# The second wave of read-back tiles placed behind the last single's loads, and its adds behind the last output

## The chip, the core and the metric

The kernel runs on one core of a Trainium2 chip. The metric is the device time of one execution in microseconds; several executions are made and the median is quoted. A profile of one further execution gives the times of single instructions; its times are counted from the start of its span.

## The reference, cut to what matters

Two layers are computed on 3327 nodes with 256 features each. A layer adds a graph convolution and then a mixture of experts to x. The end of layer 1, which is all that matters here, is this:

```python
out = tokens
for e in range(E):                                   # 8 experts, two of them chosen per token
    h = jax.nn.gelu(tokens @ w1[e] + b1[e], approximate=False)
    y = h @ w2[e] + b2[e]
    out = out + combine[:, e:e + 1] * y              # combine is zero but for the two chosen
...
x = x + _L1_ffn_ref((_layernorm(x, axis=-1))[None], ...)[0]
return x
```

Each token gets two weighted expert rows added to its row of x, and x is the result.

## The kernel before

The 3327 nodes are padded to 3328 and stand as 26 tiles of 128 rows; x stays in SBUF as [128, 26, 256]. The tokens are listed by expert in a table in DRAM (`xlist1`) and taken in blocks. A pair block has 256 tokens of one expert, a single has 128. Layer 1 runs 8 early pairs, 18 late pairs and, in the usual case, 6 singles: blocks 0 to 31 in the order in which they run, of which 26 to 31 are the singles. `layer1.step` runs a block: SP loads the tokens and the expert's first weights (lines 893, 900, 907, six blocks ahead), PE turns and multiplies them, ACT applies the GELU, PE multiplies again, and DVE adds the bias and scales by the token's weight (lines 987, 988). POOL then scatters the rows of the result to `ys1` in DRAM, one scatter for each 128 tokens (line 551). `ys1` has two rows for each token.

To finish, the two rows of every token are read back from `ys1` into the upper or lower part of a buffer of the ring (`load_outputs`, line 1050, issued by SP), DVE adds them to x in two instructions (`add_loaded`, line 1064), and x goes out to DRAM (lines 1384 and 1413). A read must not start before the scatters that fill its rows have landed. `follow` makes a read wait for a list of scatters; `outputs` holds all scatters so far. The blocks are planned so that tiles 0 to 13 have all their rows once 16 blocks are done, tiles 14 to 21 once 24 are done, and tiles 22 to 25 only with the last. (If a run's tokens don't fit this plan, another arm is taken, which the change doesn't touch.)

The loop over the steps (lines 1380 to 1402) places this work. `at` is the number of blocks begun. When `at` is 16 (`EARLY + E`), the seven pairs of tiles of the first wave are put in `waiting`, with the scatters of the first 16 blocks; when it is 24 (`EARLY + 2 * E`), the four pairs of tiles of the second wave (14 to 21), with those of the first 24. One read is placed per step, and the read is moved to `asked`; an add is placed two steps or more after its read, but, by the bound in the condition, not once `at` is over `layer1.always - FIXED[1]` = 26; the output follows a step later. The second wave's reads stand behind steps 27, 28, 29 and 30, and its adds come after the loop. There the four last tiles are read singly with all scatters as their list, and then all is added in the order of `asked`, then `left`; each add is followed by an output, from ACT, for the last tiles from ACT and SP in turn. `behind(last_y)` makes a scheduler place instructions behind the last scaling of an expert's rows on DVE.

Each engine runs its instructions in order. SP issues its transfers in order too: an instruction that waits holds up all that stand behind it. A DMA issued by SP, ACT or POOL goes on by itself and raises a semaphore when it has landed.

Of the kernel before, what the change touches and what calls it, by code (L numbers as in the profile page):

```python
# [25 lines left out]
D = 256  # L26
DC = D // P
E = 8
# [5 lines left out]
RING = 6  # L34
PIECE = CJ * PW
# [4 lines left out]
K = 2  # L40
# [18 lines left out]
EARLY = 8  # L59
# [5 lines left out]
FIXED = (4, 6)  # L65
# [13 lines left out]
BEGUN, FIRST_TILES, MORE_TILES = 12, 14, 22  # L79
# [12 lines left out]
def gnn_moe_two_layers(  # L92
# [24 lines left out]
    nc = tc.nc  # L117
# [12 lines left out]
    ring = [state.tile([P, PIECE], F32, name=f"ring{i}") for i in range(RING)]  # L130
# [93 lines left out]
    rows_written, early_rows, outputs, last_product, last_y = [], [], [], [], []  # L224
    after = mybir.DependencyInfo(mybir.DependencyClass.Sync, mybir.DependencyReason.DATA)

    def follow(later, earlier):
        for o in earlier:
            tc.add_manual_dep(later.ins, o.ins.name, after, reason="same rows of DRAM")

    def behind(instructions):

        if instructions and any(i is instructions[-1].ins for i in nc.cur_bb.bb.instructions):
            return tc.issue_after(instructions[-1].ins)
        return nullcontext()
# [31 lines left out]
    def statistics(t0, n, kept=None):  # L267


        mv, guess = kept or (  # L270
            work.tile([P, n, 2], F32, name="ln_mv"), work.tile([P, n], I32, name="ln_guess")
        )
        for g in range(n):
            st = work.tile([P, 6], F32, name="ln_st")
            nc.vector.bn_stats(out=st, in_=x[:, t0 + g, :])  # L275
            nc.vector.bn_aggr(out=mv[:, g, :], in_=st)
        ve = work.tile([P, n], F32, name="ln_ve")
        nc.vector.tensor_scalar(ve, mv[:, :, 1], EPS, None, ALU.add)  # L278
        nw = work.tile([P, n], F32, name="ln_nw")
        half = nw.bitcast(I32)  # L280
        nc.vector.tensor_scalar(half, ve.bitcast(I32), 1, None, ALU.logical_shift_right)
        nc.vector.tensor_scalar(guess, half, -1.0, float(0x5F3759DF), ALU.mult, ALU.add)
        rs = guess.bitcast(F32)
        for _ in range(3):
            nc.vector.scalar_tensor_tensor(nw, rs, -0.5, rs, ALU.mult, ALU.mult)
            nc.vector.tensor_tensor(nw, nw, ve, ALU.mult)
            nc.vector.scalar_tensor_tensor(rs, nw, 1.5, rs, ALU.add, ALU.mult)
        return mv, rs
# [149 lines left out]
    def rows_of(a, t0, n):  # L438
        return a[t0 * P : (t0 + n) * P, :].rearrange("(n p) d -> p n d", p=P)
# [609 lines left out]
    def load_outputs(yt, ys, t0, n, written, group=None):  # L1049
        d = nc.sync.dma_start(  # L1050
            out=yt,
            in_=ys[t0 * P * K : (t0 + n) * P * K, :].rearrange(
                "(n p k) d -> p n (k d)", p=P, k=K
            ),
        )
        follow(d, written)
        if group:
            tc.add_to_no_dep_group(group, d.ins)
        output_loads.append(d)

    def add_loaded(yt, t0, n):
        x_t = x[:, t0 : t0 + n, :]
        for k in range(K):
            nc.vector.tensor_tensor(x_t, x_t, yt[:, :, k * D : (k + 1) * D], ALU.add)  # L1064
# [10 lines left out]
    ys1 = dram.tile([YROWS, D], F32, name="ys1")  # L1075
# [110 lines left out]
    at = BEGUN * K * D  # L1186
# [15 lines left out]
    for t, n in FOURS:  # L1202
        if t < BEGUN:
            yt = in_s[:, t * K * D : (t + n) * K * D]
            begun.append((yt.rearrange("p (n d) -> p n d", n=n), t, n))

    def add_begun():
        for b in begun:
            add_loaded(*b)
# [44 lines left out]
    def between():  # L1254

        normal.clear()
        second.clear()
        waiting = []
        for pair in turned_pairs():
            waiting.append(pair)  # L1260
            if len(waiting) > 1:
                second_features(*waiting.pop(0))
        second_features(*waiting.pop(0))
        outputs.clear()
        rows_written.clear()

        for pan in range(ahead):
            n_loads = len(begun) + (NCHUNK if pan == 0 else 0)
            load_panel(pan, filter_behind, output_loads[0:n_loads])
# [22 lines left out]
    def new_layer1():  # L1292
        return experts(
            xlist1, ys1, "1", FIXED[1], D, AF.Gelu, f1_w1, f1_b1, f1_w2, f1_b2,
            nc.scalar.copy, kept=(EARLY // 2, w2_all, gate, f1_b1_sb),
        )
# [16 lines left out]
    def panels1(layer1, turn=False):  # L1313


        def after(pan):
            if pan < NPAN - 1:
                after1(layer1, pan)
                if turn and pan == NPAN - 2:
                    layer1.turn_first()  # L1320
            else:
                list_waiting()

        return after
# [23 lines left out]
    with tc.If(first_usual > 0) as arms:  # L1348
        output_loads.clear()
        for yt, t, n in begun:  # L1350
            load_outputs(yt, ys0, t, n, written, "read0")
        layer0.step(late)
        layer0.step(late)
        with behind(last_y):
            add_begun()
        layer0.step(late)
        with behind(last_y):
            statistics(0, BEGUN, begun_stats)
        layer0.steps_to(late, layer0.always)
        between()  # L1360
        layer1 = new_layer1()
        aggregate(gnn_b_sb, filter_chunk, panels1(layer1, True), loaded=ahead)
        late1 = first_blocks(layer1)

        layer1.steps_to(late1, EARLY - 1)
        layer1.step(late1, place=blk.tile([P, DC, SB], F32, name="xT_arms", bufs=1))
        baset, nbt = late1[4], late1[6]  # L1370
        second_usual = usual(
            [(FIRST_TILES, baset[:, E : 2 * E]), (MORE_TILES, baset[:, 2 * E :])],
            [(late1[5][0:1, :], FIXED[1])],
            nbt[:, E : 2 * E],
        )
        before_inner = layer1.state()
        with tc.If(second_usual > 0) as inner:  # L1377
            layer1.know(2 * E)
            waiting, asked, added, k = [], [], [], 0
            while len(layer1.started) < layer1.always:  # L1380
                layer1.step(late1)
                at = len(layer1.started)
                for tiles in added:
                    nc.scalar.dma_start(out=rows_of(out, *tiles), in_=x[:, tiles[0] : sum(tiles), :])
                added.clear()
                if at == EARLY + 2 * E - 2:
                    layer1.know_rest(late1)

                with behind(last_y):
                    if asked and asked[0][2] + 1 < at <= layer1.always - FIXED[1]:  # L1390
                        yt, tiles, _ = asked.pop(0)
                        add_loaded(yt, *tiles)
                        added.append(tiles)
                if waiting and at > waiting[0][1] + (1 if k < FIRST_TILES // 2 else 2):
                    tiles, _, written = waiting.pop(0)
                    yt = ring[k % RING][:, PIECE - 2 * K * D :].rearrange("p (n d) -> p n d", n=2)
                    load_outputs(yt, ys1, *tiles, written, "read1")
                    asked.append((yt, tiles, at))
                    k += 1
                if at in (EARLY + E, EARLY + 2 * E):  # L1400
                    tiles = range(0, FIRST_TILES, 2) if at == EARLY + E else range(FIRST_TILES, MORE_TILES, 2)
                    waiting.extend(((t, 2), at, list(outputs)) for t in tiles)
            assert not (waiting or added)
            left = []
            for i, t in enumerate(range(MORE_TILES, NT)):
                yt = ring[i][:, 0 : K * D].rearrange("p (n d) -> p n d", n=1)
                load_outputs(yt, ys1, t, 1, outputs)
                left.append((yt, (t, 1)))
            with behind(last_y):
                for i, (yt, tiles) in enumerate([(yt, tiles) for yt, tiles, _ in asked] + left):  # L1410
                    add_loaded(yt, *tiles)
                    queue = nc.sync if i > len(asked) and i % 2 else nc.scalar
                    queue.dma_start(out=rows_of(out, *tiles), in_=x[:, tiles[0] : sum(tiles), :])
        with inner.Else():
            layer1.back_to(before_inner)
            layer1.rest(late1)
            finish(FOURS)
    with arms.Else():
# [9 lines left out]
        layer1 = new_layer1()  # L1428
# [157 lines left out]
```

## Time and profile before

| | us |
|---|---|
| median of 7 runs | 1223.79 |
| lowest and highest of them | 1220.72, 1225.70 |
| profiled execution | 1224.16 |
| its span | 1222.44 |

The span reaches from the first to the last instruction; the execution's time is 1.72 longer. The stretches of the end, from a view that gives the busy time of each engine in each (us):

| stretch | PE | DVE | ACT | POOL | DMA share | GB/s |
|---|---|---|---|---|---|---|
| 1195 to 1198 | 2.94 | 1.02 | 1.66 | 1.68 | 0.19 | 69 |
| 1198 to 1209 | 4.63 | 6.03 | 1.86 | 3.38 | 0.84 | 272 |
| 1209 to 1217.5 | 0.00 | 5.08 | 0.00 | 0.00 | 0.78 | 241 |

SP has no row, since all it does is issue and wait. The DMA share is the mean busy share of the core's 16 DMA engines. In SP's own waits from 1193 on, most is for scatters:

```profile
SPq L1050 <- DMA ys<-wide,index: 13.2, 4, 4.2
```

The columns are the total, the number of waits and the longest one. A lowercase q behind an engine's name is its sequencer, which issues and waits.

### The profile page before, as it was taken

The numbers are of one execution on the slowest core, as the hardware profiler recorded it, in microseconds if no ns is written. First come the engines' busy times: TensorE is split into PE (matmuls) and PEld (weight loads), VectorE is DVE, ScalarE is ACT, GpSimd is POOL, SyncE is SP. The second block draws the span as 40 slices with busy tenths as digits, with TensorE's granted clock in tenths as the row PEclk, the third lists the DMA queues.
The fourth block names the chain that finished last, engine by engine and source line by source line (L and its number), as shares of the span: only waits on it lengthen the run. The fifth ranks groups of instructions, "written<-read, shape, count | busy, mean of one in ns | idle before, by whom it ended". The sixth has DMA issues, their size and how long they took to land. (4 is left out here: it accounts for less than half of the span.)

```text
span 1222.4 us, 18156 instructions
## 1 busy us (share of the span) xinstructions
PE 1190.0 (97%) x5819; PEld 1032.4 (84%) x5819; DVE 707.1 (58%) x2841; ACT 511.7 (42%) x950; POOL 270.2 (22%) x341
## 2 busy tenths in 40 slices
PE   8999999999999999999999999999999999999983
PEld 7888888888888888888888888888888888888862
DVE  7577756766583111111111177568999998886454
ACT  2655456545422222323222225896455453043321
POOL 3004111311141111011111110002323323255531
PEclk9999999999999999999999999999999999999997
DMA  9799744444358555756657657144445442477796
GB/s 342 175 311 287 214 147 169 148 156 154 100 182 263 182 185 179 262 177 225 219 194 237 230 198 283 66 168 176 163 179 187 161 170 87 122 247 231 231 290 209
DMA packets 123177, 241.59 MB, mean 198 GB/s; under 512 B 24480, under 2 KB 93120, under 8 KB 116160
## 3 DMA queue, kind: packets, MB, share of 16 engines
q1 hardware_dynamic: 108656, 205.59, 51.6%
q0 software_dynamic: 11136, 31.60, 7.1%
q10 hardware_dynamic: 3280, 3.15, 0.8%
q8 instruction: 48, 0.79, 0.3%
q14 instruction: 57, 0.47, 0.1%
HBM read 203.98 MB, written 36.33 MB: 197 GB/s over the span
## 5 line engine op out<-in xcount | busy, mean ns | idle before, releaser
L383 PE MATMUL ps_g<-ring,s 128*128 128x256 f32 x1352 | 297.0, 382 | 2.7 <-DVE s L297 2.6
L360 PE MATMUL ps_g<-s,ring 128*128 128x256 f32 x1352 | 294.2, 380 | 0.0
L383 PEld LDWEIGHTS ps_g<-ring,s 128*128 128x128 f32 x1352 | 257.5, 191 | 38.0 <-DVE s L297 3.7
L360 PEld LDWEIGHTS ps_g<-s,ring 128*128 128x128 f32 x1352 | 256.4, 190 | 33.9
L941 PE MATMUL ps_h<-xT,ring 128*128 128x256 f32 (+1 forms) x1176 | 249.3, 365 | 4.3 <-ACT xT L932 4.1
L941 PEld LDWEIGHTS ps_h<-xT,ring 128*128 128x128 f32 x1176 | 204.6, 190 | 41.3 <-ACT xT L932 5.2
L948 ACT ACTIVATE wide<-ps_h,ring 128x256 f32<-128x256 f32 (+1 forms) x240 | 110.2, 459 | 284.0 <-PE ps_h L941 283.1
L447 DVE SCALAR_TENSOR_TENSOR rt_product<-xn,gate 128x256 f32<-128x256 f32 x400 | 198.6, 496 | 12.2
L980 PE MATMUL ps_y<-ring,wide 128*128 128x256 f32 x896 | 200.4, 379 | 0.0
L551 POOL DMA_INDIRECT xlist<-xn,rt_idx x104 | 105.0, 1010 | 391.9 <-DVE ln_ve L278 154.5
L980 PEld LDWEIGHTS ps_y<-ring,wide 128*128 128x128 f32 x896 | 167.3, 190 | 20.8
L1126 ACT ACTIVATE sign<-ring,below 128x416 bf16<-128x416 f32 x208 | 133.5, 642 | 9.6 <-DMA ring<-in_adjT 3.3
L551 POOL DMA_INDIRECT ys<-narrow,index x56 | 54.8, 978 | 325.5 <-DVE narrow L988 234.2
L1275 ACT ACTIVATE ring<-ring 128x3328 f32<-128x3328 f32 x22 | 65.4, 2979 | 87.5 <-DVE ring L1274 50.6
L932 DVE COPY xT<-ptb 128x512 f32<-128x512 f32 (+1 forms) x29 | 18.9, 652 | 141.6 <-PE ptb L929 141.6
L987 DVE TENSOR_TENSOR narrow<-ps_y,ring 128x256 f32<-128x256 f32 x56 | 23.8, 424 | 131.1 <-PE ps_y L980 130.9
L512 ACT ACTIVATE rt_d<-rt_d 128x2 f32<-128x2 f32 x26 | 5.3, 203 | 162.4 <-DVE rt_d L511 162.4
L551 POOL DMA_INDIRECT ys<-wide,index x58 | 57.4, 990 | 56.1 <-DVE wide L988 31.3
L1276 ACT ACTIVATE ring<-ring 128x3328 f32<-128x3328 f32 x22 | 65.4, 2978 | 0.6
L329 DVE TENSOR_TENSOR gnn_t<-ps_o,gnn_b_sb 128x256 f32<-128x256 f32 x26 | 11.0, 424 | 82.3 <-PE ps_o L396 82.3
L980 PE MATMUL ps_y<-s,narrow 128*128 128x256 f32 (+1 forms) x200 | 48.1, 381 | 0.1
L275 DVE BATCH_NORM_STATS2 ln_st<-x 128x6 f32<-128x256 f32 x104 | 42.1, 414 | 5.7 <-DMA x<-in_x 5.1
(213 smaller groups left out, 1036.9 us busy)
## 6 DMA issues: line engine op xcount, KB each, us to landing
ring<-in_adjT SPq DMA_DIRECT2D x50, 1664.0 KB, 8.0
ring<-in_f_w1T SPq DMA_DIRECT2D x30, 1024.0 KB, 6.0
ring<-in_f_w2T SPq DMA_DIRECT2D x30, 1024.0 KB, 8.2
ring<-xlist SPq DMA_DIRECT2D x52, 258.0 KB, 2.9
ring<-in_f_w SPq DMA_DIRECT2D x36, 256.0 KB, 3.9
ring<-ys SPq DMA_DIRECT2D x12, 512.0 KB, 4.8
ring<-in_f_b SPq DMA_DIRECT2D x34, 128.0 KB, 7.8
xlist<-wide SPq DMA_DIRECT2D x16, 257.0 KB, 8.8
```

What stands on the lines that cost most here:

```text
L275: nc.vector.bn_stats(out=st, in_=x[:, t0 + g, :])
L360: nc.tensor.matmul(ps[it], lhsT=chunks[k][:, c, ts(it, P)], rhs=s[:, j, :], start=(j == 0), stop=(j == NT - 1),)
L383: nc.tensor.matmul(sums[pan][c], lhsT=s[:, j, ts(c, P)], rhs=piece(pan, j // CJ)[:, j % CJ, :], start=(j == 0), stop=(j == NT - 1),)
L447: nc.vector.scalar_tensor_tensor(product, xn[:, g, 0, 0:D], 1.0, gate[:, e, :], ALU.mult, ALU.mult, accum_out=sc[:, g, e : e + 1],)
L551: d = nc.gpsimd.indirect_dma_start(out=a[:, :], out_offset=bass.IndirectOffsetOnAxis(ap=index, axis=0), in_=rows_, in_offset=None,)
L941: nc.tensor.matmul(ps, lhsT=w1[:, c, ts(hc, P)], rhs=xT[:, c, :], start=(c == 0), stop=(c == DC - 1),)
L948: nc.scalar.activation(hT[:, hc, :], ps, func, bias=bb1[:, hc : hc + 1])
L980: last_product[:] = [nc.tensor.matmul(ps, lhsT=hT[:, hc, ts(g, P)], rhs=w2[:, hc, :], start=(hc == 0), stop=(hc == hc_n - 1),)]
L987: nc.vector.tensor_tensor(y[:, g, :], ps, bb2, ALU.add)
L1126: nc.scalar.activation(sign, piece(pan, k)[:, :, ts(i, GROUP)], AF.Sign, bias=below, accum_out=positive[:, pan, i, k : k + 1],)
L1275: nc.scalar.activation(a, a, AF.Square)
L1276: nc.scalar.activation(a, a, AF.Tanh)
```

## The change

The bound on `at` in the adds' condition goes, and so does the first wave's own spacing in the reads' condition (the second wave had another). The second wave is no longer put in `waiting`; only the list of its scatters is kept (`second_written`), as of the same step as before. Its four reads are placed after the loop, ahead of the reads of the last four tiles, with the same list and into the same buffers, and the four pairs stand first in `left`. The adds and outputs are in the same order as before, and the same two outputs go to SP.

```diff
                 with behind(last_y):
-                    if asked and asked[0][2] + 1 < at <= layer1.always - FIXED[1]:
+                    if asked and at > asked[0][2] + 1:
                         yt, tiles, _ = asked.pop(0)
                         add_loaded(yt, *tiles)
                         added.append(tiles)
-                if waiting and at > waiting[0][1] + (1 if k < FIRST_TILES // 2 else 2):
+                if waiting and at > waiting[0][1] + 1:
                     tiles, _, written = waiting.pop(0)
...
-                if at in (EARLY + E, EARLY + 2 * E):
-                    tiles = range(0, FIRST_TILES, 2) if at == EARLY + E else range(FIRST_TILES, MORE_TILES, 2)
-                    waiting.extend(((t, 2), at, list(outputs)) for t in tiles)
-            assert not (waiting or added)
+                if at == EARLY + E:
+                    waiting.extend(((t, 2), at, list(outputs)) for t in range(0, FIRST_TILES, 2))
+                if at == EARLY + 2 * E:
+                    second_written = list(outputs)
+            assert not (waiting or added or asked)
+
             left = []
+            for t in range(FIRST_TILES, MORE_TILES, 2):
+                yt = ring[k % RING][:, PIECE - 2 * K * D :].rearrange("p (n d) -> p n d", n=2)
+                load_outputs(yt, ys1, t, 2, second_written, "read1")
+                left.append((yt, (t, 2)))
+                k += 1
             for i, t in enumerate(range(MORE_TILES, NT)):
...
             with behind(last_y):
-                for i, (yt, tiles) in enumerate([(yt, tiles) for yt, tiles, _ in asked] + left):
+                for i, (yt, tiles) in enumerate(left):
                     add_loaded(yt, *tiles)
-                    queue = nc.sync if i > len(asked) and i % 2 else nc.scalar
+                    queue = nc.sync if tiles[0] >= MORE_TILES and i % 2 else nc.scalar
                     queue.dma_start(out=rows_of(out, *tiles), in_=x[:, tiles[0] : sum(tiles), :])
```

The reads still belong to the group `"read1"`, which tells the recording layer that later scatters need not wait for these reads.

## The prediction

> **What bounds the kernel now.** I read the page first, then the chain of waits, then the timeline of the last 30 us, then SP's issues one at a time, then the DMA rows.
>
> ```profile
> span 1222.4 us, 18156 instructions
> ...
> PE 1190.0 (97%) x5819; PEld 1032.4 (84%) x5819; DVE 707.1 (58%) x2841; ACT 511.7 (42%) x950; POOL 270.2 (22%) x341
> ```
>
> PE is busy for 97% of the span, so it sets nearly all of it. The change, however, touches only the end, and there the chain of waits (start, length, what) holds no PE:
>
> ```profile
> 1203.88 5.07 DMA ys<-wide,index
> ...
> 1210.92 4.76 DMA ring<-ys
> ...
> 1215.77 0.43 DVE x L1064
> ...
> 1217.04 0.43 DVE x L1064
> ```
>
> The last single's scatter is issued at 1203.88 and has landed at 1208.95. Then the rows of tiles 22 to 25 are read back, and their adds end at 1217.04 + 0.43 = 1217.47. The last output leaves after that, and 4.97 us later the span of 1222.44 ends. Whatever delays the last add, delays the end. The timeline (start, length, engine) shows what runs beside this chain:
>
> ```profile
> 1192.74 0.97 POOL L551 DMA_INDIRECT ys<-wide,index  x1 [3.44 <-DVE index L962]
> ...
> 1195.03 0.97 POOL L551 DMA_INDIRECT ys<-wide,index  x1 [1.33 <-DVE index L962]
> ...
> 1197.29 0.99 POOL L551 DMA_INDIRECT ys<-wide,index  x1 [1.29 <-DVE index L962]
> ...
> 1199.55 0.97 POOL L551 DMA_INDIRECT ys<-wide,index  x1 [1.27 <-DVE index L962]
> ...
> 1203.52 2.49 DVE L1064 TENSOR_TENSOR x<-x,ring 128x512 f32<-128x512 f32 x4
> 1203.88 1.17 POOL L551 DMA_INDIRECT ys<-wide,index  x1 [1.11 <-POOLq L1377]
> ```
>
> SP's own issues, each from a narrow window of the timeline:
>
> ```profile
> 1197.42 0.38 SPq L1050 DMA_DIRECT2D ring<-ys  x1
> ...
> 1197.91 0.41 SPq L1050 DMA_DIRECT2D ring<-ys  x1
> ...
> 1202.57 0.36 SPq L1050 DMA_DIRECT2D ring<-ys  x1
> ...
> 1204.16 0.71 SPq L1050 DMA_DIRECT2D ring<-ys  x1
> ...
> 1209.41 0.33 SPq L1050 DMA_DIRECT2D ring<-ys  x1
> ```
>
> The first four are the second wave (tiles 14 to 21, 512 KB each), the fifth is the first of the four 256 KB reads. The reader is to see that the second wave moves while the last scatters are in flight, and that its first four adds (1203.52) already run before the last scatter lands. Each of the four reads leaves just after a scatter has landed: the built instruction list gives read one a wait on the scatter of block 26 (issued at 1192.74), read two on that of 27, read three on 28, read four on 29. That is the scatter recorded just ahead of the read, one beyond the list of scatters that the code hands over.
>
> The DMA rows: landing times of these reads and of the scatters, and a stretch in layer 0 in which three 1024 KB reads of the same kind stand in a row:
>
> ```profile
> DMA to landing us min/median/max: 4.0/4.8/5.9
> ```
> ```profile
> DMA to landing us min/median/max: 2.4/3.7/6.9
> ```
> ```profile
> 686.50:695.00 8.50, 8.50 (x43) 7.47 (x42) 1.31 (x4) 0.95 (x3) 0.97 (x1) 1.00 1.01 370
> ...
> 1198.00:1209.00 11.00, 4.63 (x28) 3.59 (x27) 6.03 (x16) 1.86 (x6) 3.38 (x4) 0.83 0.84 272
> ```
>
> The last column is GB/s: 370 where only large reads stand in line, 272 in the present tail.
>
> **The change part by part.** *First wave and loop conditions:* the two conditions were already met at the same steps, so the reads of tiles 0 to 13, their adds and outputs keep their places on SP, DVE and ACT in the built lists. 0 us. Nothing is queued behind a new wait there.
>
> *The four reads of the second wave move.* SP's order stays the same: four pair reads, four single reads, two outputs. What changes is the wait. Being recorded behind the last step, the first of them now waits for the scatter of block 31, the last one; the built list has that wait, and the next three have no scatter left to wait for. Behind it on SP stand all eight reads; for them DVE waits (16 adds), and for DVE all eight outputs. So the pair reads go from 1197.42 to 1204.16 to a time after the last scatter's landing.
>
> *The last scatter itself.* PE, ACT and DVE make it at 1203.88 as before: no read or add stands in their way earlier. Its landing now has no reads or outputs beside it. The trace has no scatter in exactly that quiet, so I bound it: the scatter of 1195.03 freed a read that left at 1197.91, 2.88 later at most; the one of 1192.74, among weight loads, freed one at 1197.42, 4.68 later. I take the first, because the traffic beside it was nearest to none: first pair read at 1203.88 + 2.9 = 1206.8, against 1209.41 for the first single read today. That is a gain of 2.6 us for everything behind it.
>
> *The transfers behind it.* Before, 4 x 0.262 MB had to be read after the last scatter; now 4 x 0.524 + 4 x 0.262 = 3.15 MB. The first pair takes 4.0 (the least of the row, nothing being beside it), the other 2.62 MB at 370 GB/s 7.1: 11.1 us. Outputs share the engines: the first pair is in at 1210.8, its two adds take 2.49 / 2 = 1.25, so its output goes at about 1212.1, the next two 1.4 us apart, and these three (3 x 0.262 MB / 370 = 2.1 us) move ahead of the last read; the fourth goes too late to matter. Bounds for the outputs' share: 0 and 2.8 (all four). I take 2.1. The last read lands at 1206.8 + 11.1 + 2.1 = 1220.0, its two adds end 0.95 later (2 x 0.43, and their start): 1220.95.
>
> *DVE.* The adds no longer alternate between two pairs, so a pair's output needn't wait for the next pair's read; their number is the same. Eight adds of 0.62 and eight of 0.43 are 8.4 us: from 1210.8 on they could end at 1219.2, 1.7 before the transfers let them. Hidden; if the transfers were faster, this would be the floor.
>
> *Lanes.* In the built list the third and fourth single reads wait for the landing of pairs two and three. Pair three lands at 1210.8 + 2 x 1.42 = 1213.6; the fourth single read, 4.8 long, is then in by 1218.4. Hidden behind 1220.0.
>
> *Sum.* 1220.95 - 1217.47 = +3.5 us for the last add. From it to the end 4.97 us stay: the same output, end and barrier. The profiled execution took 1224.16 (span 1222.44 and 1.72 around it); the median shown is 1223.79. The difference goes onto the median: 1227.3.
>
> Two rules of the Trainium skill bear on this. "DMA: Bandwidth & Descriptors", section "Anatomy of one DMA", puts a DMA at some 2 us and its bytes at 436 GB/s; by that the eight reads taken as one need 2.0 + 7.2 = 9.2 us instead of 11.1, an estimate, the last would land at 1218.1, and DVE's floor would decide: +1.8. The row with 370 GB/s is of this chip and this kind of read, so I stay with it. The same page, section "Issuing engines are not separate DMA queues", says that DMAs of all issuers interleave on the same 16 engines. With it, outputs from ACT delay reads from SP; without it, rival A would be the forecast.
>
> **The rivals.** *A, smaller loss (1225.6).* The outputs delay nothing, and DVE's floor of 1219.2 plus 0.1 sets the end: +1.8 us. For it: the 370 GB/s row is a mean with a ramp of others' reads in it. Against it: with reads and outputs together, today's tail moved 272.
>
> *B, larger loss (1230.6).* The mixed traffic keeps to 272 GB/s: 2.62 + 0.79 MB take 12.5 instead of 9.2 us, +3.3, so +6.8. For it: the row itself. Against it: that stretch has idle gaps in it (busy share 0.84) while SP waited for scatters, and here all reads are queued at once.
>
> *C, faster (1222.4).* The reads would be free at block 23's scatters, the list that the code hands over, and leave from 1197.42 on, 0.5 apart, without the three later waits. The last pair would land at 1197.42 + 4.0 + 4.3 = 1205.7 rather than shortly before 1208.86, and the last scatter, with less beside it, in the median's 3.7 rather than 5.07: -1.4. It decides if the first pair read leaves before about 1200. For it: that list ends with block 23. Against it: the four reads of today each waited for the scatter recorded before them, and the built list now names the last one's.
>
> **How the numbers follow.** My forecast has 0.69, A 0.15, B 0.12, C 0.04. The likeliest one's range is from +2.5 (A's edge) to +6.0 (scatter at 4.68: +1.8; the fourth output: +0.7). About 0.2%, 2.4 us, is what a measurement of this kernel can tell. Slower: forecast and B, 0.81; same: A, 0.15; faster: C, 0.04. The range to hold 8 in 10 goes from A's lower side, 1224.9, to 1230.0; it leaves out C and most of B.
>
> **What would show it.** Right, step by step: no pair read on SP before the last scatter's landing; that scatter landing in under 3.5 us; eight reads issued within some 7 us of one another; DVE idle from 1203.6 to about 1211, then adds until about 1221; the chain of waits with the last scatter, then reads, then adds. Wrong: a pair read that leaves near 1197; a scatter as slow as 5 us although alone; DVE without gaps between its adds (then A); more than 13 us from the first read to the last landing (then B).

## The result

| | us |
|---|---|
| median after, 14 runs | 1228.12 (1226.04 to 1230.52) |
| median before beside it, 34 runs | 1224.18 |
| ratio, 95% interval | 1.003, 1.0022 to 1.0038 |
| profiled execution after, its span | 1228.76, 1226.96 |

The kernel became slower by 0.3%, some 3.7 us (2.7 to 4.7). The page of the profile after shows the same work on the engines:

```profile
span 1227.0 us, 18152 instructions
...
PE 1190.8 (97%) x5819; PEld 1033.5 (84%) x5819; DVE 707.6 (58%) x2841; ACT 511.7 (42%) x950; POOL 270.1 (22%) x341
```

The number of instructions on PE and DVE is that of before, their busy time differs by under 1 us, and the span is 4.5 longer: time has gone into waiting. SP's own waits from 1193 on (total, times, longest):

```profile
SPq L1050 <- DMA ys<-wide,index: 12.6, 1, 12.6
...
SPq L1050 <- DMA ring<-ys: 3.4, 2, 1.8
```

Four waits for scatters have become one, of 12.6 us, and all eight reads stand behind it. The second row is new: two of the single reads wait for the landing of earlier pair reads. The chain of waits of after (start, length, what):

```profile
1205.17 2.39 DMA ys<-wide,index
...
1207.69 0.38 SPq L1050
...
1209.44 6.17 DMA ring<-ys
...
1215.68 5.27 DMA ring<-ys
...
1220.97 0.43 DVE x L1064
...
1221.43 0.42 DVE x L1064
```

The last scatter is issued at 1205.17 and has landed at 1207.56. Only then does the first pair read go. The chain runs over the landing of pair three (1215.61) to the last single read, and over that read's landing at 1220.94 to the last add. DVE's timeline shows the gaps (start, length, in brackets the idle time before it and what ended it):

```profile
1204.54 0.35 DVE L988 TENSOR_SCALAR wide<-wide,ring 128x256 f32<-128x256 f32 x1
1211.25 1.42 DVE L1064 TENSOR_TENSOR x<-x,ring 128x512 f32<-128x512 f32 x2 [6.36 <-DMA ring<-ys]
1213.49 1.42 DVE L1064 TENSOR_TENSOR x<-x,ring 128x512 f32<-128x512 f32 x2 [0.82 <-DMA ring<-ys]
1215.64 1.42 DVE L1064 TENSOR_TENSOR x<-x,ring 128x512 f32<-128x512 f32 x2 [0.72 <-DMA ring<-ys]
1217.27 4.58 DVE L1064 TENSOR_TENSOR x<-x,ring 128x512 f32<-128x512 f32 x10 [0.21 <-DMA ring<-ys]
```

Before, five of the pairs' eight adds were done ahead of the last scatter's landing (1208.95); now DVE stands idle for 6.36 us and starts them at 1211.25.

From here on, *tail* means the time from the issue of the last scatter to the end of the last add, read from a profile. What made it up, in this pair of profiles and in a second one (before_again and after_again below, each from a chip of its own):

| us | before | after | before, second | after, second |
|---|---|---|---|---|
| last scatter issued to the first read that waits for it | 5.53 | 2.52 | 4.88 | 2.51 |
| that read to the last landing | 7.08 | 13.25 | 6.54 | 12.63 |
| last landing to the end of the last add | 0.98 | 0.91 | 0.98 | 1.10 |
| tail | 13.59 | 16.68 | 12.40 | 16.24 |

The scatter gives back 3.0 (2.4 in the second pair), the reads cost 6.2 (6.1). The rest of the difference between the first two spans (4.5) isn't in the tail: the last scatter was issued 1.29 later, by the clock stretch described in the last section, and 0.14 lies behind the last add.

The second profile of after differs in what sets the end. Its first read landed 5.29 us after its issue, not 3.54, and from then on DVE adds without a gap:

```profile
1225.48 8.41 DVE L1064 TENSOR_TENSOR x<-x,ring 128x512 f32<-128x512 f32 x16 [8.11 <-DMA ring<-ys]
```

There DVE's own adds set the end, not the last landing (1232.79, for adds that end at 1233.89). In the first profile both come out together: from 1217.27 on DVE adds all but without a gap as well.

### The profile page after: what moved, and what is told of

Its sections match the earlier page's. It is cut to its first block, busy times and chain, and to the rows that moved or that the text cites. A ratio compares the mean times of both kernels' runs of the same rounds, so it can differ in the third digit from the quotient of the medians.

```text
span 1227.0 us, 18152 instructions
## 1 busy us (share of the span) xinstructions
PE 1190.8 (97%) x5819; PEld 1033.5 (84%) x5819; DVE 707.6 (58%) x2841; ACT 511.7 (42%) x950; POOL 270.1 (22%) x341
```

## The experiments

Three chips were used, and their times differ by 1%; so each kernel is given by its ratio to the kernel before on its own chip, whose medians were 1235.66 (35 runs; the first four rows), 1223.37 (35 runs; the next four) and 1225.79 (17 runs; the last three). The ratio isn't the quotient of the two medians; the two differ by up to 0.0016 (after_free).

| kernel | median us | ratio, 95% interval | tail in its profile |
|---|---|---|---|
| after_again | 1239.81 | 1.0027, 1.0012 to 1.0043 | 16.24 |
| after_free | 1234.21 | 0.9972, 0.9956 to 0.9988 | 11.09 |
| before_free | 1233.93 | 0.9983, 0.9969 to 0.9998 | 11.89 |
| half | 1234.86 | 0.9996, 0.9980 to 1.0012 | 13.72 |
| before_again | 1223.07 | 0.9998, 0.9985 to 1.0011 | 12.40 |
| after_no_out | 1228.05 | 1.0028, 1.0017 to 1.0039 | 16.06 |
| after_no_read | 1222.97 | 0.9993, 0.9982 to 1.0005 | 10.86 |
| in_loop | 1224.79 | 1.0008, 0.9995 to 1.0022 | 10.05 |
| after_no_add | 1228.01 | 1.0025, 1.0016 to 1.0034 | 15.60 |
| free_both | 1216.13 | 0.9927, 0.9915 to 0.9940 | 11.25 |
| free_both_after | 1215.85 | 0.9925, 0.9912 to 0.9938 | 11.04 |

**The two kernels again.** after_again is the changed kernel as it stands, before_again the kernel before.

> The changed kernel unchanged, for a second profile: its last scatter was issued 1.29 us later than in the kernel before's profile, at 1205.17. If that is chance of one execution, here it is issued nearer 1203.9, and the span shrinks with it; if it belongs to the change, it is again at about 1205.2. From the last scatter's issue to the last add's end 16.7 us in both cases.

> The kernel before unchanged, for a second profile: where its last scatter is issued (1203.88 in the first) tells how far one execution's profile may be shifted against another's ahead of the tail. From that issue to the last add's end 13.6 us again.

The loss is there on another chip, and the second pair of profiles gives the tail 16.24 - 12.40 = 3.8 us, beside 3.1 in the first. The place of after_again's last scatter (1217.65) settles nothing, since the spans on its chip are 1% longer. A tail of the same kernel thus differs by up to 1.2 from one profile to the next; differences of tails under that are not made much of below.

**The wait for the last scatter taken away.** The code hands the second wave's reads a list that ends with block 23; the wait for later scatters is added by the layer that records the program. Here the reads are declared free of the scatters of blocks 24 to 31, in the kernel after (after_free) and in the kernel before (before_free), with the same edit:

```diff
                 tc.declare_no_dep(d.ins, group="read" + group, reason="not rows read by then")
+                if t >= EARLY + 2 * E:
+                    tc.add_to_no_dep_group("late" + group, d.ins)
                 outputs.append(d)
...
             tc.add_to_no_dep_group(group, d.ins)
+            if group == "read1" and t0 >= FIRST_TILES:
+                tc.declare_no_dep(d.ins, group="late1", reason="not rows of these tiles")
```

> The changed kernel, with the four reads of the second wave declared free of the scatters of blocks 24 to 31 (none of their rows); they keep the list of the first 24 blocks' scatters, their place behind the loop, the order of the adds and the lanes. Mine (the loss is the wait for the last scatter and the bytes that it pushes behind it): the reads leave SP right behind the singles' last load, the adds start at the last scaling again, and the time is 1221 to 1223.5. Rival (the place behind the loop, the order of the adds or the lanes cost it): it stays at 1227 to 1229.

> The kernel before with the same declaration for the second wave's reads. Mine: SP's order and waits are then those of the changed kernel with the declaration, so both are equal within 1 us, 1221 to 1223.5, and below the kernel before, since each of its reads waited for the scatter recorded just ahead of it. Rival (place and order matter): this one at 1222, the other at 1228.

With this edit alone the changed kernel goes from 1.0027 to 0.9972, 5.6 us by the medians, and its tail from 16.24 to 11.09. SP's timeline of after_free shows where the reads went (the second row spans six of the eight, from the first to the last issue):

```profile
1209.38 0.33 SPq L907 DMA_DIRECT2D ring<-in_f_b  x1
1209.88 13.41 SPq L1052 DMA_DIRECT2D ring<-ys  x6
```

They leave right behind the last single's loads, 9.1 us ahead of the last scatter (1219.00), as the diff's placement has it. On DVE all eight pair adds then follow the last scaling without a gap:

```profile
1218.37 0.35 DVE L988 TENSOR_SCALAR wide<-wide,ring 128x256 f32<-128x256 f32 x1
1218.64 4.90 DVE L1068 TENSOR_TENSOR x<-x,ring 128x512 f32<-128x512 f32 x8
```

before_free and after_free have overlapping intervals. So the place of the reads in the program costs nothing measurable (the intervals leave room for 1 us or so); the wait that comes with the place makes the loss.

**Half of the move.** Two of the four pairs stay in the loop, and two go behind it:

```diff
-BEGUN, FIRST_TILES, MORE_TILES = 12, 14, 22
+BEGUN, FIRST_TILES, HALF, MORE_TILES = 12, 14, 18, 22
...
-                    tiles = range(0, FIRST_TILES, 2) if at == EARLY + E else range(FIRST_TILES, MORE_TILES, 2)
+                    tiles = range(0, FIRST_TILES, 2) if at == EARLY + E else range(FIRST_TILES, HALF, 2)
...
+            for t in range(HALF, MORE_TILES, 2):
+                yt = ring[k % RING][:, PIECE - 2 * K * D :].rearrange("p (n d) -> p n d", n=2)
+                load_outputs(yt, ys1, t, 2, second_written, "read1")
...
```

> Of the four pairs of the second wave the first two are read as before (steps 27 and 28), the last two behind the loop as in the change. Mine (bytes behind the last scatter, 2.1 instead of 3.15 MB, and two outputs fewer): 2.8 to 3.5 us below the changed kernel, 1224.5 to 1225.5. Rival (a fixed cost of waiting for the last scatter, however little is behind it): 1227 to 1228.

Moving half costs nothing that can be told from zero (at most 1.5 us by the interval), where half of the full loss would be 1.8. Beside after_again it is 3.8 us lower by the ratios, a little more than was expected. The trace offers a reason why the loss isn't shared out evenly: the last scatter already has quiet and frees the first read 2.60 after its issue, so the whole gain of that step is had (5.53 - 2.60 = 2.9), and it pays for two pair reads. The other two, moved as well, have nothing left to pay for them.

**The outputs taken away, then the adds too.**

```diff
                     queue = nc.sync if tiles[0] >= MORE_TILES and i % 2 else nc.scalar
-                    queue.dma_start(out=rows_of(out, *tiles), in_=x[:, tiles[0] : sum(tiles), :])
+                    if tiles[0] >= MORE_TILES:
+                        queue.dma_start(out=rows_of(out, *tiles), in_=x[:, tiles[0] : sum(tiles), :])
```

> The changed kernel without the four outputs of tiles 14 to 21 (these rows of the result are left out). Mine: outputs share the DMA engines with the reads and cost 2.1 us of the tail; without them the last read lands about 2 us sooner and DVE's adds set the end: 1225.4 to 1226.6. Rival (outputs go beside the reads at no cost): 1227.5 to 1228.5.

```diff
                 for i, (yt, tiles) in enumerate(left):
+                    if tiles[0] < MORE_TILES:
+                        continue
                     add_loaded(yt, *tiles)
```

> The changed kernel with the adds and the outputs of tiles 14 to 21 left out (these rows of the result are missing); the four reads stay. Without their outputs alone the end of the adds moved by 0.4 us though the last read landed 1.2 us sooner. Mine now (DVE's adds, started late, had become the bound there): the last read lands 11.7 us after the first as there, its adds follow at once, the last add ends 15.0 to 15.4 us after the last scatter's issue, 0.7 to 1 below the kernel without the outputs: 1226.5 to 1227.3 where the kernel before has 1224. Rival (DVE never bound it): 16.0 and the same time as without the outputs.

Neither gave time back: 1.0028 and 1.0025 stand beside 1.003. In the first, the reads need 11.73 from the first issue to the last landing instead of 13.25, but DVE takes the gain over. Its timeline:

```profile
1211.94 1.42 DVE L1064 TENSOR_TENSOR x<-x,ring 128x512 f32<-128x512 f32 x2 [6.64 <-DMA ring<-ys]
1214.29 7.34 DVE L1064 TENSOR_TENSOR x<-x,ring 128x512 f32<-128x512 f32 x14 [0.93 <-DMA ring<-ys]
```

After 1214.29 the adds run to 1221.63 with one gap of 0.14, while the last read had landed at 1219.83. DVE is the limit there; its adds and the two waits among them take 9.7 us. Without the adds, the last landing is as far behind the scatter as without the outputs (14.2 in both), and the tail is 15.60:

```profile
1216.05 3.27 DVE L1064 TENSOR_TENSOR x<-x,ring 128x256 f32<-128x256 f32 x8 [12.61 <-DMA ring<-ys]
```

By the tails the outputs are worth 0.6 and the adds 0.5 more; by the times neither can be told from nothing. So these two runs don't separate the adds' part from the outputs', and they show that the wait and the four reads make nearly the whole loss even without the pairs' adds and outputs.

**The reads taken away.** The adds stay, but nothing is read for tiles 14 to 21:

```diff
             for t in range(FIRST_TILES, MORE_TILES, 2):
                 yt = ring[k % RING][:, PIECE - 2 * K * D :].rearrange("p (n d) -> p n d", n=2)
-                load_outputs(yt, ys1, t, 2, second_written, "read1")
                 left.append((yt, (t, 2)))
```

> The changed kernel without the four reads of the second wave (the adds of tiles 14 to 21 take what is in the buffers). Mine: only 1.05 MB are read behind the last scatter, the pairs' adds run from the last scaling on, and the last add ends some 7.5 us sooner than in the change: 1219.5 to 1222. Rival (the order of the adds or the place of the outputs sets it): 1225 to 1228.

The loss is gone (0.9993), but the further gain that was expected isn't there. Part of that is in DVE's timeline:

```profile
1206.83 4.90 DVE L1064 TENSOR_TENSOR x<-x,ring 128x512 f32<-128x512 f32 x8
1213.23 0.88 DVE L1064 TENSOR_TENSOR x<-x,ring 128x256 f32<-128x256 f32 x2 [1.51 <-DMA ring<-ys]
```

The pair adds run at once, so their four outputs are issued from 1208.74 to 1211.76, beside the single reads, which then take 7.08 from the first issue (1210.06) to the last landing, as long as before. The tail is 10.86, 2.7 under the first profile of before and 1.5 under the second; the time is only 0.8 lower (2.2 lower to 0.6 higher). What became of the rest, 1 to 2 us, stays open.

**The second wave's adds put into the singles' steps.** before_free, with the loop's two conditions as the change has them, so that the adds and outputs no longer wait for the end of the loop:

```diff
-                    if asked and asked[0][2] + 1 < at <= layer1.always - FIXED[1]:
+                    if asked and at > asked[0][2] + 1:
...
-                if waiting and at > waiting[0][1] + (1 if k < FIRST_TILES // 2 else 2):
+                if waiting and at > waiting[0][1] + 1:
```

> The kernel before with the reads declared free of later scatters and without the bound in the adds' condition: the second wave's adds and outputs run in the steps of the last singles, the last two of them ahead of or between the last single's bias and scaling. Mine: behind the last scatter only the four last tiles are left; it is issued up to 1.4 us later, and the time is 1218 to 1221. Rival (DVE becomes the bound of the singles' steps, at about 1.1 + 1.25 us in 2.26): 1222 to 1225.

The tail is the shortest of all, 10.05, and yet the time isn't below that of before. POOL's timeline shows the price:

```profile
1198.04 0.99 POOL L551 DMA_INDIRECT ys<-wide,index  x1 [4.02 <-DVE index L962]
1201.92 1.17 POOL L551 DMA_INDIRECT ys<-wide,index  x1 [2.90 <-DVE wide L988]
1205.80 1.17 POOL L551 DMA_INDIRECT ys<-wide,index  x1 [2.71 <-DVE wide L988]
```

The scatters are 3.9 apart instead of 2.26. Adds that wait for their reads (4.4 us in all from 1196 to 1208) now stand in DVE's order ahead of the indices and the scaling of the next singles, and in this profile the granted clock is at 0.5 from 1197.1 to 1204.0 besides. The last scatter goes at 1207.88, and what the tail gained is lost ahead of it; how much of that is the adds' and how much the clock's isn't told apart.

**Both waves freed.** The first wave's reads wait in the same way for scatters beyond their list. They are declared free of blocks 16 to 31, the second wave's of 24 to 31, on the kernel before (free_both) and on the kernel after (free_both_after):

```diff
+                if t >= EARLY + E:
+                    tc.add_to_no_dep_group(("late" if t >= EARLY + 2 * E else "mid") + group, d.ins)
...
+            if group == "read1":
+                tc.declare_no_dep(d.ins, group="late1", reason="not rows of these tiles")
+                if t0 < FIRST_TILES:
+                    tc.declare_no_dep(d.ins, group="mid1", reason="not rows of these tiles")
```

> The kernel before with the reads of both waves declared free of the scatters that hold none of their rows: blocks 16 to 31 for the first wave, 24 to 31 for the second. Mine: DVE no longer waits for the first wave's last read, a wait that held up the first single by about 2.6 us, so PE's idle stretch there shrinks, and the time is 1218 to 1221 where the kernel before has 1224. Rival (the wait is for the transfer itself, or the second wave's first read now holds up the last singles' loads on SP): 1222 to 1224.

> The changed kernel with the same declarations for both waves: its second wave stands behind all loads on SP. Mine: like the other with both waves free, or up to 1.5 us below it where that one's reads hold up loads: 1217.5 to 1220.5 where the kernel before has 1224. Rival: 1221 to 1223, as with the second wave alone.

Both beat the kernel before by some 0.74% (1225.79 x 0.0074 = 9 us), more than was expected, and they don't differ from each other: with no false wait, the change costs nothing that can be told from zero. What DVE waited for reads from 1100 on (total, times, longest) shows the other half of the gain. In before:

```profile
DVE x L1064 <- DMA ring<-ys: 15.7, 11, 3.1
```

In free_both_after:

```profile
DVE x L1070 <- DMA ring<-ys: 3.1, 3, 2.5
```

Those waits stood in the steps, in DVE's order, ahead of the experts' scaling. Without them the last scatter is issued at 1198.2 instead of 1203.9 (1202.8 in the second profile of before, which is from another chip), and the tail is 11.0 to 11.3 instead of 12.4 to 13.6. The clock has a part in this gain: over all runs on this chip its mean is 0.9940 and 0.9938 in the two kernels and 0.9905 before, and a tail 1 to 2.5 us shorter at 0.50 makes only 0.0005 to 0.001 of that. How much of the 9 us is the clock's isn't told apart.

## Why the prediction held

The forecast was 1227.3, +3.5 us, and the measured ratio is +3.7 (2.7 to 4.7). The wait that it named as the cause is shown by after_free: take the wait for the last scatter away, and leave all else in its place, and the loss is gone with more. What it put behind that wait was right in the sum, but partly by errors that cancel, and in the second profile another term than the forecast one set the end. Step by step:

*The loop conditions, 0.* Held: the first wave's instructions keep their places, and the scatter of block 27 goes at 1195.03 before and at 1195.01 after; the traces part behind it, with the clock stretch told of below.

*The last scatter in quiet, first read 2.9 later.* 2.52 in the profile, 2.51 in the second one. The 2.88 of before was an upper bound: that scatter had itself landed 2.45 after its issue (1197.48), and the read that waited for it stood behind another on SP. Gain 3.0 rather than 2.6 against the same profile of before.

*The reads, 4.0 + 7.1 = 11.1 without outputs.* 11.7 in both experiments without outputs. The first landing came sooner there (3.5 and 3.8, but 5.29 in the second profile of after), and the other 2.62 MB then took 7.9 and 8.2 us, which is 331 and 322 GB/s, not 370. The rate of a row with three large reads beside weight loads was too good for eight smaller ones.

*The outputs, 2.1.* Mis-sized: 13.25 - 11.73 = 1.5, and 12.63 - 11.73 = 0.9 in the second profile. The first three pairs' outputs move ahead of the last read as said, but they take less than their own transfer time. And their removal doesn't bring the end forward, since DVE stands close behind. The two errors, reads too short and outputs too long, cancel, and that is luck: 13.2 was predicted from the first read to the last landing, and 13.25 and 12.63 were found.

*DVE's floor, 8.4 from the first landing, 1.7 of room.* The floor came out: 8.41 in the second profile of after, again by two errors that cancel (5.39 for the eight pair adds, not 4.96, and 3.02 for the eight single ones, not 3.44). The 0.62 was taken from a row (four adds in 2.49) in which the adds of two pairs alternate. Now the two adds of one pair stand together, and the second starts 0.73 after the first (1211.25 and 1211.98 in after). The room was not as forecast: DVE's waits behind its first add are 0.82 + 0.72 + 0.21 = 1.75 in the first profile, but all lie ahead of 1217.27, so an earlier last landing would have brought the end forward by some 0.2 at most; in the second there are none. There the sum is 2.5 to the first read, 5.3 to its landing and 8.4 of adds: nearly the size of the forecast, by another way.

*Lanes, hidden.* (A lane here is a semaphore that two reads share: the later one waits for the earlier one's landing.) The waits were those named: reads seven and eight left at 1213.53 and 1215.68, as pairs two and three landed (1213.47 and 1215.61; 1213.6 was foreseen for pair three, and 1218.4 for the landing of a read that came at 1220.94). The chain of waits passes through the second. It cost the end little: from 1217.27 on DVE stands idle by some 0.2 in the first profile, and not at all in the second. In after_no_out the lanes fell otherwise, these reads left at 1212.41 and 1212.98, so the 1.5 between the landings of the two kernels holds both the outputs and this.

*The end part, 4.97.* 5.11 (5.46 in the second profile; 4.82 in the second one of before).

*The rivals.* C is out: no pair read left before 1207.69. What it described is after_free, which had to be told that the reads are free, and there it gains. B's rate of 272 is near the mean over the whole stretch (290 GB/s from 1207 to 1222.1), but B's extra 3.3 ask for 16.5 from the first read to the last landing, and 13.25 and 12.63 were found. A's size (+1.8) lies outside the interval; its mechanism, DVE's floor as the bound, is what the second profile of after shows, with a first landing 1.3 later than the 4.0 of the forecast. So transfers as the sole bound, which the forecast had and A denied, aren't shown.

*The signs named beforehand.* No pair read before the scatter's landing, a scatter under 3.5 us, DVE idle from 1204.9 to 1211.25, and the order in the chain are as said. The eight reads were issued within 8.0 us of one another, not 7, for the lanes. The sign for B, over 13 us from the first read to the last landing, was badly set: the forecast itself stood at 13.2. The sign for A, DVE without gaps between its adds, is missing in the first profile and is there in the second.

The Trainium skill's "DMA: Bandwidth & Descriptors", section "Anatomy of one DMA", gave 9.2 us for the eight reads as one transfer. That section's fit is for transfers that GpSimd issues, one at a time, and these are eight that SP issues; the runs without outputs show 11.7, and the measurement decides. Its section "Issuing engines are not separate DMA queues" agrees with the 0.9 to 1.5 us by which the last read lands later when outputs issued by ACT run beside the reads issued by SP, though part of that may be the lanes'.

## What to carry to other kernels

Where a read is placed decides which writes it is made to wait for, whatever list the code hands over: look for the wait in the built program, and compare in the trace when a read leaves with when its last needed write has landed. If it waits for more than it needs, free it before moving it: here the move cost 0.3%, freeing the moved reads gained 0.5% against that, and freeing those ahead of them as well gained 0.7% against the kernel before. When work is gathered behind one late event, price the transfers behind it with the rate of transfers of their own size, and work out the next engine's floor, since that takes over what a cheaper transfer would give.

## What the runs showed of the hardware

**A pause of PE, and the clock at half for 3.41 us.** In both profiles PE pauses in the step of the first single, behind an add that waits for its read. In after:

```profile
1192.51 0.44 PE L929 MATMUL ptb<-ident,ring 128*128 128x128 f32 x2 [2.81 <-ACT narrow L948]
```

The granted clock is the column before the last two (DMA share, GB/s). In after, behind that pause:

```profile
1193.60:1197.00 3.40, 3.40 (x15) 3.20 (x14) 1.00 (x4) 1.11 (x3) 0.98 (x2) 0.50 0.81 251
```

The same stretch of before, behind a pause of 2.65:

```profile
1193.60:1197.00 3.40, 3.34 (x24) 2.90 (x22) 1.77 (x7) 1.41 (x4) 1.07 (x2) 1.00 0.62 204
```

Half the clock, and 15 matmul records instead of 24: one step of the singles took 3.57 us (1195.01 to 1198.58) instead of 2.26, and the last scatter went 1.29 later. Of the 13 profiles, 6 have such a stretch in these steps (both of after, but neither of before; after_no_add, with the changed reads, none); five are 3.41 long, and that of in_loop is 6.83. The programs are the same up to there, so nothing shows that it belongs to the change. The clock over whole runs speaks against a large share in the loss: its mean is 0.9878 in after_again and 0.9890 before on the same chip, and a tail 3 to 4 us longer at 0.50 lowers it by 0.0012 to 0.0016 by itself. The standard error of the difference, 0.0006, leaves room for about 1 us.

The traces also show what the length of the pause alone doesn't. In all 13 the clock changes only on a grid of 3.41 us, which lies elsewhere in each run. Counted on this grid from 30 us on, every stretch at full clock in which PE was idle for 2.0 us or more was followed by one at 0.50, and none with less than 1.87; four lie from 1.87 to 1.94, and one of these was (some 4500 stretches in all). In after, 2.30 of the pause fall into one stretch (3.41 less 1.11 of PE, the number behind the comma):

```profile
1190.21:1193.62 3.41, 1.11 (x6) 1.00 (x7) 2.35 (x8) 1.00 (x3) 0.97 (x1) 1.00 0.95 281
```

In before a border of the grid divides the pause, and no stretch has more than 1.6 of idle time:

```profile
1188.12:1191.53 3.41, 1.83 (x13) 1.53 (x11) 1.28 (x3) 0.37 (x1) 0.97 (x1) 1.00 0.96 306
1191.53:1194.95 3.42, 2.29 (x15) 1.99 (x16) 2.06 (x10) 1.48 (x5) 0.97 (x1) 1.00 0.89 266
```

The Trainium skill's "TensorE: Matmul & The Clock Gate", section "Part 1: The HAM clock gate", has a free-running window of 3413 ns and half the clock after at least one idle window. The grid agrees with that window, but here 2.0 us of idle time in one were enough, and the measurement decides.

**A scatter's landing depends on what is beside it.** The last scatter needed 5.07 us beside reads and outputs (before; 4.42 in its second profile), 2.39 alone (after and after_again, and 2.38 in after_no_out). Moving transfers away from it gave back 3.0 of the 6.2 us that they cost.

**One part in sixteen lands late.** A transfer raises its semaphore in 16 parts. The scatter of block 30 in after had 15 of them by 1205.48 and the last at 1207.04, when hardly anything else was moving (61 GB/s from 1198 to 1207). The same scatter has such a late part in after_no_out (1205.89 and 1207.08) and after_no_add (1204.02 and 1205.07). In the second profile of after it is the first read that has one: 15 parts by 1223.42 and the last at 1225.45, and DVE stood waiting for it. What holds it up isn't known.
